# A hybrid block on one core: the order of copies and convolution taps, one buffer moved from the gated outputs to the gates, and a hand-written order for the first and last blocks

## The chip, the cores and the metric

The kernel runs on one NeuronCore of a Trainium2 chip. The metric is the device time in microseconds; a run's time is given as the median of several executions. The engines named below are TensorE (PE, matrix products and transposes), VectorE (DVE), ScalarE (ACT), GpSimd (POOL) and SyncE (SP, which issues most of the DMAs). SBUF is the on-chip memory[...], and PSUM is the memory that matrix products are written to.

## What is computed

Four residual steps on an input x of 4 x 256 rows of 512 columns: attention with an adapter, a feed-forward layer with a selection of rows and columns, a state-space mixer, and the feed-forward layer once more. Nearly all of the time, and all of the change, lies in the mixer and in its seams to the layers before and after it. Of the reference, cut to the mixer:

```python
proj = input_states @ in_proj_w.T                       # gate | x, B, C | dt
gate = proj[..., :INTER]                                # INTER = 128 heads x 64 = 8192
xBC = proj[..., INTER:INTER + CONV]
dt = proj[..., INTER + CONV:]
xBC = silu(depthwise_conv(xBC, conv_w, 4 taps) + conv_b)
hs, Bm, Cm = split(xBC)                                 # 8 groups of B and C, 128 wide
dt = softplus(dt + dt_bias)
cum = cumsum(dt * A)                                    # A = -exp(A_log), one per head
y[i] = sum_{j <= i} (C_i . B_j) * exp(cum_i - cum_j) * dt_j * hs_j  + D * hs_i
g = y * silu(gate)
g = g * rsqrt(mean over the 1024 columns of a group of g*g + eps) * norm_w
out = g @ out_w.T
```

The reference writes the sum over j in chunks with a carried state; the kernel computes it over pieces of 64 rows.

## The kernel before

The 8192 inner columns are cut into 64 blocks of 128 columns, two heads each; eight blocks form a group, which shares one B and one C. All 1024 rows lie along the free axis of a tile, so a block's projection is a 128 x 1024 tile in PSUM. Each float32 product is made from three products of rounded high parts and remainders (`mm3`, lines 115 to 117), so that every weight is split into a high part (a copy on ACT) and a remainder (a subtraction on DVE or POOL).

**One block.** `block(i)` (line 1316) issues, as one step of a software pipeline, work of several blocks. In order of the text:

- the spill of the gated output of block i-2 to DRAM (`spilled`, line 1133), issued from ACT's DMA queue;
- the first half of the projection of x(i) on PE (`projected`, `project`);
- `decays(i-1)`: for two heads, the exponentials of the differences of `cum` on ACT (`exponentials`, line 1070), seven activations each;
- where the projection of B or C for the next group is waiting (blocks 4 and 5 of a group, since `NEXT = {3: "b", 4: "c"}` places these projections at the end of blocks 3 and 4), `conv` of it: a copy with scale and bias on ACT (line 995) and three taps on DVE (line 1002), 1024 columns each, all reading the projection from PSUM;
- `turn(i-1)`: eight transposes of x on PE (line 1096) into two PSUM tiles `trx`, and two copies on DVE into `xd`, multiplied by dt (line 1099); `weigh(i-1)`: the exponentials times the scores, two DVE products `em` (line 1089);
- the second half of x(i), its `conv` on ACT and DVE, the square of block i-2 on ACT and its sum on POOL (`squared`, line 1140);
- `outer`: from group 1 on, a product with the output weights for one tile of 128 rows of the previous group, 24 matmuls into a PSUM tile `pog`;
- silu of x(i) into `x2`, the remainders of the weights fetched, the projection of the gate g(i), the inner products of block i-1 (`product`, 64 small matmuls into `pyy`, and `gated`, lines 1122 to 1131, into a tile `gb`), the differences of block i (`differences`, line 1058, on DVE), and silu of the gate into `gt` (line 1407, ACT).

For ACT, DVE, PE and POOL the loop over the 64 blocks is under `tc.manual_schedule`: each of these engines executes its instructions in exactly the order of the text, one after the other, and an instruction that has to wait holds up all that stands behind it on its engine. SP's DMAs are ordered by the planner. Everything outside that loop is ordered by the planner, which works from its own estimates.

**Buffers.** A tile asked for with a tag takes one of `bufs` buffers, and waits until one is released by all its readers and writers. [...]the projections share two tiles of two banks each (tag `pp`), `pyy` has two banks, and `trx`, `pog` and the scores `pg` share two tiles of one bank each (tag `m` of pool `ps`). In SBUF, B and C after the convolution share the tag `gb` with the gated outputs, four buffers of 128 x 1024; `gt` has one. `em` has three, two being made per block.

**The first blocks.** The projections of dt and of B's first block are made together with the norm before (`first`, line 863). Then lines 911 to 973 compute softplus of dt (exp, a logarithm, and a small series for small values, lines 935 to 938), the running sums `cum` by a scan, store them to DRAM for later loads of single rows (`rows`, line 1045), and transpose `cum`, its suffixes and dt into `col_t`, `end_t` and `dt_t`. Lines 1258 to 1271 follow with the convolutions of B and C of group 0, their scores (`scores`, line 1020: matmuls on PE, masked copies `gm` on DVE) and the first rows. All of this is ordered by the planner together with the first part of block 0.

**The end.** After block 63, lines 1420 to 1441 finish blocks 62 and 63 and the last outer product of group 6, split the output weights of group 7, and begin the output products of the last group for the first four row tiles (`begun`: the half of the sum over blocks 56 to 59). The loop from line 1460 adds the other half, then the feed-forward layer runs. This end is ordered by the planner too.

Of the kernel before, what the change touches and what calls it, by code (L numbers as in the profile page):

```python
# [12 lines left out]
I32 = mybir.dt.int32  # L13
# [66 lines left out]
def hybrid_kernel(  # L80
# [705 lines left out]
    def mixer(feed, later):  # L786
        with ExitStack() as es, ExitStack() as inner:
# [126 lines left out]
            col_t = w1.tile([P, H, TT], F32, name="col_t")  # L914
            end_t = w1.tile([P, H, 4], F32, name="end_t")
            dt_t = w1.tile([P, TT, H], F32, name="dt_t")

            pp = first[0]
            reset = p2.tile([P, NT], F32, name="reset", tag="sq", bufs=1)[:, :512]
            nc.gpsimd.memset(reset, 1.0)  # L920
            nc.gpsimd.memset(reset.rearrange("p (c i) -> p c i", i=P)[:, :, 0:1], 0.0)
            hs = [slice(half * 512, half * 512 + 512) for half in range(2)]
            dtile = lambda n, j: [
                po_.tile([P, 512], F32, name=f"{n}{i}", tag=f"wo{j}", bufs=GB) for i in range(2)
            ]
            vs, es2, lgs, ss = dtile("dv", 0), dtile("de", 0), dtile("dl", 1), dtile("dsr", 1)
            for v, e, h in zip(vs, es2, hs):
                nc.scalar.activation(v, pp[:, h], AF.Identity, bias=dtb_s)
                nc.vector.scalar_tensor_tensor(e, v, -1.0, v, ALU.mult, ALU.min)
            for e in es2:  # L930
                nc.scalar.activation(e, e, AF.Exp)
            for e, lg in zip(es2, lgs):
                nc.scalar.activation(lg, e, AF.Ln, bias=ones[:, 0:1])

            for s, e in zip(ss, es2):
                nc.vector.tensor_scalar(s, e, 1.0 / 3.0, -0.5, ALU.mult, ALU.add)
                nc.vector.tensor_tensor(s, s, e, ALU.mult)
                nc.vector.scalar_tensor_tensor(s, s, 1.0, e, ALU.add, ALU.mult)
            pair = lambda v: v.rearrange("p (k u i) -> p k u i", u=2, i=Q)
            das, natural = dtile("dda", 1), dtile("dc", 0)  # L940
            dts, cums = (p2.tile([P, NT], F32, name=n, tag="x2", bufs=2) for n in ("ddt", "dcum"))
            suf = po_.tile([P, 512], F32, name="dsuf", tag="wo1", bufs=GB)
            for u, (s, e, lg, v, da, nat, h) in enumerate(zip(ss, es2, lgs, vs, das, natural, hs)):
                small = da.bitcast(I32)
                nc.vector.tensor_scalar(small, e, 0.01, None, ALU.is_lt)
                nc.vector.copy_predicated(lg, small, s)
                apart = lambda t: t.rearrange("p (k i) -> p k i", i=Q)
                dt, cum = pair(dts)[:, :, u], pair(cums)[:, :, u]
                nc.vector.scalar_tensor_tensor(dt, apart(v), 0.0, apart(lg), ALU.max, ALU.add)
                nc.vector.tensor_scalar(apart(da), dt, 0.0, a_s, ALU.max, ALU.mult)  # L950
                nc.vector.tensor_tensor_scan(nat, reset, da, 0.0, ALU.mult, ALU.add)
                load(cumd[:, h], nat)
                nc.scalar.copy(cum, apart(nat))

                first_ = apart(nat).rearrange("p (j c) i -> p j c i", j=2)[:, :, :2]
                nc.vector.tensor_tensor(
                    pair(suf).rearrange("p (j c) u i -> p j c u i", j=2)[:, :, :, u],
                    first_[:, :, 1:2, Q - 1 : Q].to_broadcast([P, 2, 2, Q]), first_, ALU.subtract,
                )
            for j in range(2):  # L960
                qs = slice(j * 4, j * 4 + 4)
                tr = ps.tile([P, 4, P], F32, name="trd", tag="m")
                for c in range(4):
# [590 lines left out]
```

## Time and profile before

| | us |
|---|---|
| median of 3 runs | 1909.61 (1905.4 to 1910.39) |
| the profiled execution | 1907.48 |
| its span, first to last instruction | 1905.7 |
| from the first block's gate (block 0) to that of block 8 | 419.2 to 570.7 |
| one group, gate of its first block to that of the next group's (groups 2 to 6) | 181.1 |
| a block with nothing added, gate to gate, in group 3 | 19.79 |
| the blocks behind B and C in group 3, gate to gate | 29.36 and 28.17 |
| last gate (block 63) | 1802.5 |

The profile lists, for every engine, its instructions with start and duration, and for every idle stretch the instruction that ended it. "Gate" is the activation of line 1407, one per block, a handy mark for a block's end. The granted clock is the share of full speed at which TensorE was allowed to run. The lines of the profile that carry the argument are shown in the prediction.

### The profile page before, as it was taken

To read this page: it belongs to the slowest core of one execution; us is meant where nothing else is said; L and a number is where in the kernel's file an instruction comes from. 1 tells how busy PE (TensorE), PEld (TensorE's weight loads), DVE (VectorE), ACT (ScalarE), POOL (GpSimd) and SP (SyncE) were. 2 spreads that over 40 slices of the span, in tenths; PEclk is the share of its full clock that TensorE was granted. 3 is DMA by queue.
4 is the path that set the end of the run, shared out by engine and by line. 5 is a ranking of instruction groups with operands and counts; after the bars stand their busy time and mean duration, and the time that the engine had idled before them with its cause. 6 is when DMAs were issued, how large, how long until landed. Compare 5 with 4: busy or idle time off the path is not lost.

```text
span 1905.7 us, 33071 instructions
## 1 busy us (share of the span) xinstructions
PE 1798.6 (94%) x12882; PEld 1463.3 (77%) x12882; DVE 1449.3 (76%) x2158; ACT 1280.1 (67%) x2520; POOL 246.7 (13%) x251
## 2 busy tenths in 40 slices
PE   7999988889899999999999999999999999999997
PEld 6777767767677778877887888788778877888786
DVE  5566667677787777868886887878778877788776
ACT  6566675467677657766765687578666766776853
POOL 6332230000010111101101110111101011111100
PEclk9999999899999999999999999999999999999999
DMA  4000000112224223432342343234232522343231
GB/s 142 1 1 1 22 15 24 46 56 100 75 93 154 91 82 119 130 100 89 119 135 69 100 154 107 78 96 143 94 94 89 167 88 84 115 135 110 79 113 49
DMA packets 134381, 169.71 MB, mean 89 GB/s; under 512 B 12240, under 2 KB 77392, under 8 KB 134224
## 3 DMA queue, kind: packets, MB, share of 16 engines
q1 hardware_dynamic: 125152, 134.57, 23.2%
q10 hardware_dynamic: 9072, 33.03, 4.5%
q8 instruction: 101, 1.65, 0.4%
q14 instruction: 56, 0.46, 0.1%
HBM read 131.90 MB, written 35.65 MB: 88 GB/s over the span
## 4 chain that ended last, share of the span: by engine, by line
PE 68%; ACT 14%; DVE 13%; issue 3%; POOL 1%; DMA 1%; ACTq 0%; SPq 0%; DVEq 0%; POOLq 0%
PE pp L115 10%; PE pp L116 9%; PE pp L117 9%; PE pyy L1115 7%; PE pog L115 6%; PE pog L116 6%; PE pog L117 6%; DVE bc L1002 3%; ACT em L1076 3%; ACT e L477 2%; PE trx L1096 2%; DVE acc L1002 2%; ACT L1076 1%; DVE em L1089 1%; ACT em L1083 1%
## 5 line engine op out<-in xcount | busy, mean ns | idle before, releaser
L115 PE MATMUL pp<-mx,w 128*128 128x512 f32 (+1 forms) x1160 | 466.5, 402 | 7.7 <-DVE bc L1002 7.2
L117 PE MATMUL pp<-mx,w 128*128 128x512 f32 (+1 forms) x1160 | 454.0, 391 | 5.1 <-DVE w L830 5.1
L116 PE MATMUL pp<-mx,w 128*128 128x512 f32 (+1 forms) x1160 | 453.5, 391 | 0.0
L1148 POOL TENSOR_TENSOR sq<-sq,x 128x1024 f32<-128x1024 f32 x55 | 131.7, 2394 | 1284.1 <-ACT x L1147 1284.1
L1089 DVE TENSOR_TENSOR em<-em,gm 128x1280 f32<-128x1280 f32 x128 | 213.9, 1681 | 87.3 <-ACT em L1084 87.3
L115 PEld LDWEIGHTS pp<-mx,w 128*128 128x128 f32 x1160 | 219.5, 189 | 54.0 <-issue 4.2
L117 PEld LDWEIGHTS pp<-mx,w 128*128 128x128 f32 x1160 | 219.2, 189 | 51.2 <-DVE w L830 5.5
L116 PEld LDWEIGHTS pp<-mx,w 128*128 128x128 f32 x1160 | 219.7, 189 | 40.8 <-issue 0.3
L1002 DVE SCALAR_TENSOR_TENSOR acc<-pp,cw_s,acc 128x1012 f32<-128x1012 f32 (+2 forms) x192 | 244.5, 1273 | 5.1 <-ACT acc L995 0.7
L115 PE MATMUL pog<-wo,gh 128*128 128x512 f32 x512 | 206.4, 403 | 28.8 <-DVE xd L1099 27.4
L116 PE MATMUL pog<-wo,gh 128*128 128x512 f32 x512 | 204.1, 399 | 0.0
L117 PE MATMUL pog<-wo,gh 128*128 128x512 f32 x512 | 203.8, 398 | 0.0
L1014 ACT ACT_TABLE_LOAD x63 | 80.8, 1283 | 164.5 <-DVE acc L1002 164.4
L1407 ACT ACTIVATE gt<-pp 128x1024 f32<-128x1024 f32 x64 | 65.8, 1028 | 175.1 <-PE pp L117 147.3
L1115 PEld LDWEIGHTS pyy<-em,xd 64*64 64x64 f32 x4096 | 136.6, 136 | 54.0 <-DVE em L1089 16.9
L1115 PE MATMUL pyy<-em,xd 64*64 64x256 f32 (+3 forms) x4096 | 166.0, 305 | 11.1 <-DVE em L1089 11.0
L1076 ACT ACTIVATE em<-r,end_t 128x128 f32<-128x128 f32 x512 | 163.3, 389 | 0.8
L1099 DVE TENSOR_TENSOR xd<-trx,dt_t 128x512 f32<-128x512 f32 x128 | 82.3, 685 | 81.8 <-PE trx L1096 81.8
L115 PEld LDWEIGHTS pog<-wo,gh 128*128 128x128 f32 x512 | 98.6, 193 | 54.6 <-DVE xd L1099 32.7
L1002 DVE SCALAR_TENSOR_TENSOR bc<-pp,cw_s,bc 128x1012 f32<-128x1012 f32 (+2 forms) x48 | 61.2, 1275 | 99.6 <-ACT bc L995 98.5
L477 ACT ACTIVATE e<-sc,nmx 128x256 f32<-128x256 f32 (+1 forms) x256 | 104.0, 441 | 21.0 <-DVE nmx L471 20.9
L117 PEld LDWEIGHTS pog<-wo,gh 128*128 128x128 f32 x512 | 98.6, 193 | 21.1
(295 smaller groups left out, 3221.0 us busy)
## 6 DMA issues: line engine op xcount, KB each, us to landing
wr<-in_win_dram SPq DMA_DIRECT2D x145, 256.0 KB, 2.7
r<-cumd SPq DMA_DIRECT2D x256, 128.0 KB, 2.9
spill<-gb ACTq DMA_DIRECT2D x63, 512.0 KB, 2.8
gr<-spill SPq DMA_DIRECT2D x120, 256.0 KB, 3.4
wor<-in_wout_dram SPq DMA_DIRECT2D x64, 256.0 KB, 4.4
out_dram<-x SPq DMA_DIRECT2D x8, 256.0 KB, 2.4
x<-in_x_dram SPq DMA_DIRECT2D x1, 1536.0 KB, 8.7
gr<-spill SPq DMA_DIRECT2D x8, 192.0 KB, 2.6
```

The costliest lines, as they stand in the source:

```text
L115: nc.tensor.matmul(o, lh, rh, start=(first and k == 0), stop=False)
L116: nc.tensor.matmul(o, lh, rl, start=False, stop=False)
L117: nc.tensor.matmul(o, ll, rh, start=False, stop=(last and k == n - 1))
L477: nc.scalar.activation(es_[c][:, 2 * j + pr, :], sc[:, j, :], AF.Exp, bias=nm[:, j : j + 1], accum_out=rs[:, c, h : h + 1],)
L1002: nc.vector.scalar_tensor_tensor(av[:, :, d:], pv[:, :, : L - d], cw_s[:, ch, tap : tap + 1], av[:, :, d:], ALU.mult, ALU.add,)
L1014: nc.scalar.activation(pair(x2).rearrange("p k u i -> p u k i"), acc.rearrange("p (u k i) -> p u k i", u=2, i=Q), AF.Silu,)
L1076: nc.scalar.activation(piece(e, j, c, 2 - c, 2), rv[:, j, 2:, :], AF.Exp, bias=end_t[:, h, 2 * j + c : 2 * j + c + 1],)
L1089: nc.vector.tensor_tensor(e, e, gm, ALU.mult)
L1099: nc.vector.tensor_tensor(xd[:, hs, :].rearrange("p c (h d) -> p c h d", h=2), tr.rearrange("p c (h d) -> p c h d", h=2), dt_t[:, hs, 2 * ...
L1115: nc.tensor.matmul(py[d, u, j * L + c * Q : (j + 1) * L].rearrange("p (k i) -> p k i", i=Q), xd[us, 4 * j + c, d], piece(es2[hh], j, c)[us ...
L1148: (nc.gpsimd if n < NB - 1 else nc.vector).tensor_tensor(sqs[g], sqs[g], x2, ALU.add)
L1407: nc.scalar.activation(gts[i], pp, AF.Silu)
```

## The change

1. **Taps behind the copies.** `conv` is cut into `conv` (the copy on ACT) and `taps` (three operations on DVE). In `block`, the copies of a waiting B or C stay where they were, and their taps come after `turn(i-1)` and `weigh(i-1)`.
2. **Buffers.** Tag `gb` has three buffers, `gt` has two.
3. **The first blocks.** The dt work becomes a generator `steps()` in four parts, which `started()` and block 0 call at fixed places; `started()` and all blocks are under the manual schedule. In block 0 both halves of the gate's projection and the dt transposes come ahead of silu of x; the scores of group 0 move into block 1, and block 1 makes both halves of g(1) before its inner products. Of the small series of dt, one half goes to POOL, and its last operation on two inputs and a constant becomes two operations. `col_t` and `end_t` are laid out with the head as the last axis, so that the copies out of PSUM write in one piece.
4. **The end.** Block 63 makes the last outer product of group 6 after its inner products and ahead of g(63), splits four of the last group's output weights, and loads and splits the first three half tiles of the last group. Then, still under the manual schedule, come the decays, the transposes and the weighing of block 63, the output products `begun` for three row tiles, the other four weights, the inner products of block 63, and the fourth `begun`.

The diff, cut to its core:

```diff
-            col_t = w1.tile([P, H, TT], F32, name="col_t")
-            end_t = w1.tile([P, H, 4], F32, name="end_t")
+            col_t = w1.tile([P, TT, H], F32, name="col_t")
+            end_t = w1.tile([P, 4, H], F32, name="end_t")
...
+            def steps():
...
+                for v, e, h in zip(vs, es2, hs):
+                    nc.scalar.activation(v, first[0][:, h], AF.Identity, bias=dtb_s)
+                    nc.vector.scalar_tensor_tensor(e, v, -1.0, v, ALU.mult, ALU.min)
+                yield
...
+                for s, e, engine in zip(ss, es2, (nc.vector, nc.gpsimd)):
+                    engine.tensor_scalar(s, e, 1.0 / 3.0, -0.5, ALU.mult, ALU.add)
+                    engine.tensor_tensor(s, s, e, ALU.mult)
+                    engine.tensor_scalar(s, s, 1.0, None, ALU.add)
+                    engine.tensor_tensor(s, s, e, ALU.mult)
+                yield
...
+                yield
+                for v, n, end, func in ((cums, 4, col_t, AF.Copy), (suf, 2, end_t, AF.Copy), (dts, 4, dt_t, AF.Relu)):
+                    for j in range(2):
+                        tr = ps.tile([P, n, P], F32, name="trd", tag="m")
...
+                        nc.scalar.activation(end[:, n * j : n * j + n, :], tr, func)
+                yield
...
-                    else po_.tile([P, NT], F32, name="bc", tag="gb", bufs=4)
+                    else po_.tile([P, NT], F32, name="bc", tag="gb", bufs=3)
                 )
                 nc.scalar.activation(
                     acc, pp, AF.Identity, bias=cb_s[:, ch : ch + 1], scale=cw_s[:, ch, 3:4]
                 )
+                return acc
+
+            def taps(acc, pp, ch):
+
                 av = acc.rearrange("p (b t) -> p b t", b=B)
...
+            def started():
+
+                prepare(2)
+                next(dt_steps)
+                pieces.pop(0)
+                group["b"] = conv(first[1], NB, False)
+                taps(group["b"], first[1], NB)
+                next(dt_steps)
+                prepare(3)
+                fetch(6)
+                pp = whole(projected("c", 0))
+                group["c"] = conv(pp, NB + G, False)
+                silu(group["b"])
+                next(dt_steps)
+                taps(group["c"], pp, NB + G)
+                rr.update((h, rows(h)) for h in range(2))
...
                 for k in waiting:
-                    group[k] = conv(group.pop(k + "pp"), (NB if k == "b" else NB + G) + g + 1, False)
+                    group[k] = conv(group[k + "pp"], (NB if k == "b" else NB + G) + g + 1, False)
+                if i == 1:
+                    next(x_steps)
+                    scoring = scores(group.pop("b"), group.pop("c"))
+                    gms[0] = next(scoring)
+                    for _ in scoring:
+                        pass
                 if i:
                     turn(i - 1)
                     weigh(i - 1)
-                acc = conv(next(x_steps), i, True)
+                for k in waiting:
+                    taps(group[k], group.pop(k + "pp"), (NB if k == "b" else NB + G) + g + 1)
+                if i != 1:
+                    next(x_steps)
+                acc = conv(pp, i, True)
+                taps(acc, pp, i)
...
+                g_steps = projected("g", i)
+                if i == 0:
+                    pp = whole(g_steps)
+                    next(dt_steps)
+                    silu(group["c"])
                 xs2[i] = side_by_side(acc)
...
+                both = i == NB - 1
+                if i:
                     next(g_steps)
-                if i:
+                    if not done:
+                        pp = next(g_steps)
+                    if i == 1:
+                        next(g_steps)
                     inner_products(i - 1)
-                if done:
-                    next(g_steps)
+                    if both:
+                        done = outer(G - 2, TT - 1)
+                    if done:
+                        pp = next(g_steps)
...
+                if both:
+                    scaled(*done)
+                    for k in range(4):
+                        upper_out(g * GB + k)()
+                    begin(0)
+                    begin(1)
+                    begin(2)
...
-                gts[i] = p2.tile([P, NT], F32, name="gt", tag="gt", bufs=1)
+                gts[i] = p2.tile([P, NT], F32, name="gt", tag="gt", bufs=2)
...
+            def begin(t):
+                begins[t] = parts(G - 1, t, 0)
...
+                started()
                 for i in range(NB):
                     block(i)
...
+                es_p.close()
+                ps_o = pool("m_o", 4, space=PSUM, **freed)
+                i = NB - 1
+                spilled(i - 1, gbs[i - 1])
+                decays(i)
+                turn(i)
+                weigh(i)
+                for t in range(3):
+                    begun(t)
+                begin(3)
+                lower = [upper_out(i - 3 + k) for k in range(4)]
+                squared(i - 1, xs2.pop(i - 1), gbs.pop(i - 1))
+                inner_products(i)
+                for f in lower:
+                    f()
+                spilled(i, gbs[i])
+                squared(i, xs2.pop(i), gbs.pop(i))
+                begun(3)
```

## The prediction, made before the changed kernel was run

> **What bounds the kernel now.** I read first the page's busy line and its chain, then the list of what TensorE (PE) waited for in each stage of the mixer, then one block in order of time on PE, VectorE (DVE) and ScalarE (ACT), and last the granted clock in the stretches after those waits.
>
> ```profile
> PE 1798.6 (94%) x12882; PEld 1463.3 (77%) x12882; DVE 1449.3 (76%) x2158; ACT 1280.1 (67%) x2520; POOL 246.7 (13%) x251
> ...
> PE 68%; ACT 14%; DVE 13%; issue 3%; POOL 1%; DMA 1%; ACTq 0%; SPq 0%; DVEq 0%; POOLq 0%
> ```
>
> PE holds the chain over most of the span. In the mixer (436 to 1790 us) its waits are few and of one kind:
>
> ```profile
> PE pog L115 <- DVE xd L1099: 27.1, 12, 2.6
> PE pyy L1115 <- DVE em L1089: 8.7, 7, 2.0
> PE pp L115 <- DVE bc L1002: 7.2, 2, 3.8
> ```
>
> Columns: total us, times, longest. The twelve are two per group in groups 1 to 6: the block behind the projection of B and the block behind that of C. Here is one (group 3, behind C): DVE first, then PE.
>
> ```profile
> 1036.36 3.90 DVE L1002 SCALAR_TENSOR_TENSOR bc<-pp,cw_s,bc 128x1012 f32<-128x1012 f32 x3 [7.16 <-ACT bc L995]
> 1040.17 1.28 DVE L1099 TENSOR_TENSOR xd<-trx,dt_t 128x512 f32<-128x512 f32 x2
> 1041.37 4.80 DVE L1089 TENSOR_TENSOR em<-em,gm 128x1280 f32<-128x1280 f32 x2
> 1046.09 3.89 DVE L1002 SCALAR_TENSOR_TENSOR acc<-pp,cw_s,acc 128x1012 f32<-128x1012 f32 x3
> ...
> 1038.30 0.39 PE L117 MATMUL pp<-mx,w 128*128 128x512 f32 x1
> 1040.91 0.50 PE L115 MATMUL pog<-wo,gh 128*128 128x512 f32 x1 [2.22 <-DVE xd L1099]
> ```
>
> DVE stands idle for 7.16 us at the head of the taps of C, because ACT comes to C's copy (L995) only after the fourteen activations of two heads' decays. The copies of x (xd) are queued behind those taps although their transposes ended at 1035.9. The output product needs a PSUM buffer that only xd frees, so PE stops.
>
> The stop costs more than itself:
>
> ```profile
> 985.00:1000.00 15.00, 15.00 (x120) 12.21 (x120) 13.41 (x17) 9.42 (x12) 2.41 (x1) 1.00 0.35 110
> 1011.00:1019.00 8.00, 7.46 (x28) 5.75 (x32) 7.96 (x6) 2.15 (x4) 2.38 (x1) 0.79 0.00 0
> 404.00:409.00 5.00, 0.55 (x3) 0.13 (x1) 5.00 (x8) 0.25 (x1) 0.00 (x0) 0.94 0.29 105
> 409.00:416.00 7.00, 6.10 (x21) 4.29 (x21) 2.66 (x5) 2.77 (x5) 0.00 (x0) 0.56 0.31 112
> ```
>
> The third number from the right is the granted PE clock: 1.00 in a dense stretch, 0.79 behind the wait at 1009 us, 0.56 behind an idle of 5.1 us at the start. After the wait the 24 output matmuls took 7.3 us in six of the twelve blocks and 5.67 us in the other six.
>
> **What the Trainium skill says.** "TensorE: Matmul & The Clock Gate", What's actually happening: the clock goes to half after an idle window, read in free-running windows of about 3.4 us, so it depends on where the wait falls. The trace agrees: 7.3 against 5.67 us behind the same 2.2 us wait. "SBUF — State Buffer", SBUF: two separate sides: a DVE operation with two SBUF inputs and a GpSimd (POOL) operation exclude each other for a whole instruction. The trace agrees: two em products take 2.9 us alone and 4.80 above, where POOL's square sum of 2.4 us runs; the taps, with one PSUM input, stay at 1.28. "ScalarE: Activation LUTs", What ACT_TABLE_LOAD costs: 1283 ns for the load and about as much for a drain. The trace has the 1283 and no drain beside it (load 420.25 to 421.53, next activation at 421.54), so 1.28 is used.
>
> **The change part by part.** The sum is made against the profiled run: 1907.5 us, its span 1905.7; the median of the three is 1909.6, 2.1 above, within their spread of 5.
>
> *Middle: taps behind the copies, groups 1 to 6.* DVE now does xd (1.28), em, em (1.49 each), then the three taps of C (3.85), then those of x. With the times above: xd 1035.6 to 1036.9, the first em to 1038.4, the second (its exponential ended at 1035.2) to 1039.9, C's taps to 1043.8, x's taps to 1047.7 (was 1050.0). The em products now end before POOL's sum starts (1041). PE runs on: output product 1038.7 to 1044.2, pyy to 1046.6, then the gate projection, which needs the PSUM buffer that C's taps give back at 1043.8: 2.8 us to spare. In place of the projection waiting 2.2 us nothing is late; at B's block the same sum gives the buffer at 1014.2 against a need at 1017.1. PE alone needs 25.24 us from gate to gate here (a plain block of 19.79 plus 24 matmuls at 0.2275). It took 29.3 and 27.75. So 4.1 + 2.5 = 6.6 us per group, of which 4.5 is waiting and 1.6 the half clock; six groups 39.6. I take 38, because a restart of 0.1 to 0.2 us may remain. Below: 27, the waits alone; 15 if another wait takes half their place.
>
> *Group 0.* It has no output product to fill PE; one block takes 16.38 us and runs in a ring: exponentials 5.34, em 1.58, taps 3.85, table and silu 2.3, w 0.5, wait 0.33 for gb, gate silu 1.03, table 1.28, and 0.17 of gaps. Two gate buffers remove the 0.33 in about five blocks: 1.7. In blocks 4 and 5 (behind B, C) the taps of x end 2.5 to 3.9 us earlier, but B's and C's taps end 1.6 later (483.3 against 481.7), and PE's gate projection waits for them: 3.3 and 3.85 us now, 4.8 and 4.9 then. PE sets the gate there: without a clock loss the two blocks gain 2 together, with half clock behind both (the skill's window is shorter than such a wait; the second has 0.76 already) they lose 2 to 3. I take -0.7, sum +1; bounds -4 and +4. The gate's other waits for gb (27.8 us of ACT in all) are hidden by PE and cost nothing.
>
> *Start.* The dt work is cut into four steps in the order of the text, and the blocks follow it. Walking DVE from its start at 386.9 with the rows' durations: de to 388.7, B's taps 392.6, one half of the small series 394.6 (its twin of four operations goes to POOL: two of 1.29 and two bounded by 0.5 (a memset) and 1.3, done by 396.2 at the latest, needed at 398), the two halves of step 3 to 401.4, C's taps 405.2, x's 409.0, w 409.6, differences 411.6. PE: c, x(0), g(0) back to back to 404.2, then twenty transposes in six groups; ACT evacuates them by 408.0 (col_t and end_t are now written in one piece: 0.6 as dt_t, not 1.0), then silu of C and x, w, gate at 411.6 (was 420.2), exponentials to 418.2 (was 426.9). Of the 8.7 some goes back, since the score products move into block 1 between x's projection and the transposes: PE x(1) 409.7 to 415.2, scores to 418.4, xd 420.6, em 423.5, taps of x(1) 427.3 against 432.2. Gain 4.9. POOL's prepare(3) stands behind its four operations and ends at 397.5; g(0) needs it at 398.7. SP must store the scan and load two rows between 401 and 409.6: 2.0 + 2.9 us. If PE's sparse transposes bring the half clock, x(1) costs 2.5 more. I take 4.5; bounds 0 and 8.
>
> *End.* The last outer product moves ahead of g(63), and 36 output matmuls stand before pyy(63). Before: PE waited 0.35, 1.32 and 2.22, and pyy ran at a clock of 0.50, 4.54 us instead of 2.4; the group's square sums began at 1828.4. New, from pyy(62) at 1795.25: outer to 1800.8, g to 1806.3, transposes 1807.2, three half products 1815.4. ACT's gate is queued behind the third load of spilled rows (its buffer comes back at 1805, 3.4 us to land): 1808.8, exponentials to 1816.4, em 1818.0, so pyy ends at 1820.4. The fourth half product ends at 1823.1; gb and four weight remainders end at 1825.6, the square sum at 1826.8. 1.6 earlier; I take 1.5; bounds -6 (two waits at half clock) and +5.
>
> *The rest.* gb with three buffers: while B and C hold two, gb(4) takes the third, from gb(3), whose square ends at 1040.9 and whose spill lands 2.8 us after 1027; it is written after 1050. Nothing. The new layout of col_t and end_t is read through the same counts of elements: nothing.
>
> Sum: 38 + 1 + 4.5 + 1.5 = 45. **1907.5 - 45 = 1862.5; I forecast 1862.**
>
> **Rivals.** *A, half the wait comes back under another name* (em, or the PSUM buffer of B and C, with 2.8 us to spare): the middle gives 15, so 1907.5 - 22 = 1885.5. For it: two em products against POOL's sum could cost 1.8 each. Against: in the walk they end 1.1 us before POOL starts. *B, start and end in fixed order lose what the middle gives:* start -3, group 0 -4, end -3, middle 38: 1879.5. For it: waits of 4.8 us on PE in blocks 4 and 5, and ACT's gate behind a load at the end. Against: the walks above. *C, slower:* B's and C's projections hold their PSUM buffer so long that the gate projection waits in all fourteen blocks. It starts to cost at 2.8 us over my walk and eats everything at about 6.6 over; at 9 us over, 12 x 2.9 = 35 us, less 7 for the rest, 1935. For it: group 0 shows that very wait (7.2 us). Against: there PE had no output product in between. *D, the buffers were no real limit and PE still waits:* about 1905; against it, the transposes end 4 us before xd.
>
> **Numbers.** Forecast 0.63, A 0.14, B 0.12, C 0.08, D 0.03. The range 1848 to 1883 holds the forecast's bounds (middle 27 to 40, start 0 to 8, end -6 to 5, not all at their worst) and B, and about half of A. About 0.3% (6 us) can be told from no change: faster 0.88, same 0.03, slower 0.09.
>
> **What would show it.** The row pog <- xd should vanish from PE's waits, the blocks behind B and C take 25.3 us from gate to gate, the group 174.5 instead of 181.1, with a clock of 1.00. The first gate silu should fall at 411 to 414. A wait of pp <- bc in groups 1 to 6 would make A or C right; the gate of block 5 later than its distance to block 3 before (50.1 us) would make B right.

## The result: 1875.25 us, and where the 33 us come from

The changed kernel takes 1875.25 us (median of four runs, 1874.66 to 1875.91); the kernel before took 1908.63 beside it (1905.40 to 1910.39). The ratio is 0.9827, with a 95% interval from 0.9810 to 0.9844: 33 us faster. The forecast was 1862, with a range from 1848 to 1883. The profiled execution has a span of 1874.1 us against 1905.7 before, 31.6 less, and the table below accounts for these 31.6.

From the page after, the busy line and the shares of the chain:

```profile
PE 1792.8 (96%) x12882; PEld 1463.0 (78%) x12882; DVE 1428.6 (76%) x2156; ACT 1275.4 (68%) x2518; POOL 252.1 (13%) x255
...
PE 80%; DVE 8%; ACT 7%; issue 2%; POOL 1%; DMA 1%; SPq 0%; DVEq 0%; ACTq 0%; POOLq 0%
```

PE has 12 points more of the chain, DVE and ACT have 5 and 7 fewer. The two longest rows of PE's waits in the mixer say why (total us, times, longest):

```profile
PE pp L115 <- DVE bc L1006: 9.8, 2, 4.9
PE pyy L1118 <- DVE em L1092: 7.8, 4, 2.0
```

The first row of before, twelve waits of the output product for `xd` with 27.1 us in all, is gone. In groups 1 to 6 nothing new stands in its place, and from gate 8 to gate 56 the granted clock is 1.00. The row that was third, the gate projection waiting for the taps of B and C, has grown from 7.2 to 9.8 us; both its waits are in group 0.

Here is the place that the prediction walked, group 3 behind C, first on DVE, then on PE (the first matmul of each run of equal ones):

```profile
1024.02 1.29 DVE L1102 TENSOR_TENSOR xd<-trx,dt_t 128x512 f32<-128x512 f32 x2 [5.40 <-PE trx L1099]
1025.23 2.88 DVE L1092 TENSOR_TENSOR em<-em,gm 128x1280 f32<-128x1280 f32 x2
1028.03 3.90 DVE L1006 SCALAR_TENSOR_TENSOR bc<-pp,cw_s,bc 128x1012 f32<-128x1012 f32 x3
1031.84 3.89 DVE L1006 SCALAR_TENSOR_TENSOR acc<-pp,cw_s,acc 128x1012 f32<-128x1012 f32 x3
```

```profile
1027.00 0.39 PE L115 MATMUL pog<-wo,gh 128*128 128x512 f32 x1
1032.53 2.41 PE L1118 MATMUL pyy<-em,xd 64*64 64x256 f32 x64
1034.87 0.50 PE L115 MATMUL pp<-mx,w 128*128 128x512 f32 x1
```

`xd` now comes first, and its idle time is a wait for the transposes, which is work that PE does then. The output product starts without a bracket, so it waited for nothing. The taps of C end at 1031.93 (1028.03 and 3.90), and the gate projection needs their buffer at 1034.87: 2.9 us to spare, where the walk had 2.8. The two `em` products take 2.88 together in place of 4.80, since POOL's square sum (1029.49 to 1031.9) now lies beside the taps. That saving on DVE is not what ends PE's stop: before, PE had no wait for `em` behind B or C (between gate 8 and gate 56 it had two, at 577 and 580 us). The gate's activation shows the pace; the three rows are blocks 3, 4 and 5 of group 3:

```profile
990.19 1.03 ACT L1442 ACTIVATE gt<-pp 128x1024 f32<-128x1024 f32 x1 [3.74 <-PE pp L117]
1015.42 1.03 ACT L1442 ACTIVATE gt<-pp 128x1024 f32<-128x1024 f32 x1 [0.74 <-PE pp L117]
1040.65 1.03 ACT L1442 ACTIVATE gt<-pp 128x1024 f32<-128x1024 f32 x1 [1.02 <-PE pp L117]
```

From gate to gate 25.23 and 25.23 us, against 29.36 and 28.17 before; the prediction had 25.24 as the time that PE alone needs.

The gates cut the whole mixer into stages. The marks are the start of dt's first activation (`dv`), of the gate of block 1, of block 8 (the first of group 1), of block 56 (the first of the last group), and the end. All in us, from the profiled executions:

| Stage | before | after | gain | the prediction's term |
|---|---|---|---|---|
| start of the span to `dv` | 386.2 | 388.9 | -2.7 | none |
| `dv` to gate 1 (start) | 49.4 | 50.5 | -1.1 | +4.5 |
| gate 1 to gate 8 (group 0) | 135.1 | 138.0 | -2.9 | +1 |
| gate 8 to gate 56 (middle) | 1089.6 | 1048.8 | +40.8 | +38 |
| gate 56 to the end (end) | 245.4 | 247.9 | -2.5 | +1.5 |
| sum | 1905.7 | 1874.1 | +31.6 | +45 |

Up to `dv` the two programs do the same work. Over the fourteen profiled executions of this study `dv` starts anywhere between 386.0 and 389.8; the two ends of this range are two programs below that differ only from block 4 on. So the first row is taken as chance, and the times below are read from `dv` on. Three of the four parts that the change touches come out lower than forecast, and the one that carries the gain comes out higher.

### The profile page after: what moved, and what is told of

It reads as the page before. It is cut to its first block, busy times and chain, and to the rows that moved or that the text cites. A ratio compares the mean times of both kernels' runs of the same rounds, so it can differ in the third digit from the quotient of the medians.

```text
span 1874.1 us, 33084 instructions
## 1 busy us (share of the span) xinstructions
PE 1792.8 (96%) x12882; PEld 1463.0 (78%) x12882; DVE 1428.6 (76%) x2156; ACT 1275.4 (68%) x2518; POOL 252.1 (13%) x255
## 4 chain that ended last, share of the span: by engine, by line
PE 80%; DVE 8%; ACT 7%; issue 2%; POOL 1%; DMA 1%; SPq 0%; DVEq 0%; ACTq 0%; POOLq 0%
PE pp L115 14%; PE pp L117 13%; PE pp L116 13%; PE pyy L1118 8%; PE pog L115 6%; PE pog L117 6%; PE pog L116 6%; PE trx L1099 3%; ACT e L477 2%; PE ptr L493 1%; PE pq L115 1%; PE pg L1036 1%; DVE acc L1006 1%; PE pq L116 1%; PE pq L117 1%
## 5 line engine op out<-in xcount | busy, mean ns | idle before, releaser
L1006 DVE SCALAR_TENSOR_TENSOR acc<-pp,cw_s,acc 128x1012 f32<-128x1012 f32 (+2 forms) x192 | 244.6, 1274 | 7.2 <-ACT acc L995 2.6
L1092 DVE TENSOR_TENSOR em<-em,gm 128x1280 f32<-128x1280 f32 x128 | 188.7, 1489 | 70.8 <-ACT em L1087 70.8
L115 PE MATMUL pog<-wo,gh 128*128 128x512 f32 x512 | 202.3, 395 | 2.3 <-ACT gh L1209 1.3
L117 PE MATMUL pog<-wo,gh 128*128 128x512 f32 x512 | 200.8, 392 | 0.8 <-DVE gh L1214 0.8
L116 PE MATMUL pog<-wo,gh 128*128 128x512 f32 x512 | 200.3, 392 | 0.0
L115 PEld LDWEIGHTS pog<-wo,gh 128*128 128x128 f32 x512 | 96.8, 189 | 22.8 <-ACT gh L1209 1.8
L117 PEld LDWEIGHTS pog<-wo,gh 128*128 128x128 f32 x512 | 96.7, 189 | 21.4 <-DVE gh L1214 1.1
L116 PEld LDWEIGHTS pog<-wo,gh 128*128 128x128 f32 x512 | 96.8, 189 | 19.5
```

The source lines that it names most:

```text
L115: nc.tensor.matmul(o, lh, rh, start=(first and k == 0), stop=False)
L116: nc.tensor.matmul(o, lh, rl, start=False, stop=False)
L117: nc.tensor.matmul(o, ll, rh, start=False, stop=(last and k == n - 1))
L1006: nc.vector.scalar_tensor_tensor(av[:, :, d:], pv[:, :, : L - d], cw_s[:, ch, tap : tap + 1], av[:, :, d:], ALU.mult, ALU.add,)
L1092: nc.vector.tensor_tensor(e, e, gm, ALU.mult)
```

## The experiments

The theory after the result: the order of the taps alone makes the gain. Start, group 0 and end each give something back: the start to a small series split over DVE and POOL and to PE at half clock, group 0 to the half clock behind its two waits, the end to a load that is queued ahead of the last gate. The rival: the parts need one another (without the second gate buffer or the fixed order the middle would gain less), and the missing 13 us are chance or lie elsewhere.

### The taps alone

```diff
                 for k in waiting:
-                    group[k] = conv(group.pop(k + "pp"), (NB if k == "b" else NB + G) + g + 1, False)
+                    group[k] = conv(group[k + "pp"], (NB if k == "b" else NB + G) + g + 1, False)
                 if i:
                     turn(i - 1)
                     weigh(i - 1)
-                acc = conv(next(x_steps), i, True)
+                for k in waiting:
+                    taps(group[k], group.pop(k + "pp"), (NB if k == "b" else NB + G) + g + 1)
+                pp = next(x_steps)
+                acc = conv(pp, i, True)
+                taps(acc, pp, i)
```

The rest is as in the kernel before (with `conv` cut in two): start, end, four buffers `gb`, one `gt`.

> The kernel before, with nothing changed but the place of the taps of B and C behind the copies of x. Theory (the order alone gives the middle, 40 us; group 0 pays back 3 to 4): 1871 to 1873, and the row pog <- xd gone from the waits of TensorE. Rival (the two gate buffers are needed for it, since the gate would still wait for gb): 1882 or more, with a new wait in groups 1 to 6.

Measured: 1867.27 us, ratio 0.9793 (0.9779 to 0.9808). That is about 4 us below the expected range. Gate 8 to gate 56 takes 1048.1 us, the gain of the full change and 0.7 more. The two longest rows of PE's waits in the mixer:

```profile
PE pp L115 <- DVE bc L1006: 9.8, 2, 4.9
PE pyy L1119 <- DVE em L1093: 9.0, 6, 2.2
```

The twelve waits for `xd` are gone here too; one of 0.3 us is left, at the end. The move of the taps is the whole gain, and all the rest of the change together costs 6.5 us by the two ratios, 8 by the medians. From `dv` on: start 49.2 (after 50.5), group 0 136.8 (138.0), end 244.6 (247.9). Not all of this is the order: block 3's gate to block 5's took 51.8 us here and 53.9 in the full change, with the same two waits of 4.9 us in both. Behind them the granted clock was 0.79 and 0.75 here (8.0 and 8.5 us), 0.63 and 0.67 there.

### The buffers alone

```diff
-                    else po_.tile([P, NT], F32, name="bc", tag="gb", bufs=4)
+                    else po_.tile([P, NT], F32, name="bc", tag="gb", bufs=3)
...
-                gb = po_.tile([P, NT], F32, name="gb", tag="gb", bufs=4)
+                gb = po_.tile([P, NT], F32, name="gb", tag="gb", bufs=3)
...
-                gts[i] = p2.tile([P, NT], F32, name="gt", tag="gt", bufs=1)
+                gts[i] = p2.tile([P, NT], F32, name="gt", tag="gt", bufs=2)
```

> The kernel before with three buffers for gb and two for gt. Theory (the gate's waits for gb are hidden but for 0.33 us in some blocks of group 0): 1906 to 1908, the twelve waits pog <- xd unchanged at 2.2. Rival (they carry a part of the middle): 1900 or less. Slower by over 2 us would mean that the third gb buffer is missed.

Measured: 1907.3 us, ratio 0.9996 (0.9988 to 1.0005), no change that can be measured. In the profile the plain blocks of group 0 come 15.95 apart in place of 16.38, the 0.43 of which the prediction counted 0.33. That is 1.3 us from gate 0 to gate 8, less than the interval can tell. The middle stays at 1089.7.

### How much of the wait was clock

The kernel before, with nine extra matmuls ahead of the output product in the blocks behind B and C. They run in PE's wait, nobody reads them, and they are work added.

```diff
+                if waiting and g:
+                    warmed(ps_y.tile([P, NT], F32, name="warm", tag="pyy")[:, :512], [xs[0][:, 0, :P].bitcast(F32)] * 9)
                 done = outer(*out) if out and not first_out else None
```

> The kernel before with nine small matmuls, whose results nobody reads, put on TensorE into each of the twelve waits of 2.2 us. Theory (six of the twelve waits trip the clock to half, 1.6 us each): 1898 to 1900, and all twelve output products at 5.6 to 5.7 us. Rival (the 7.3 us of six of them are not from the clock): 1908 to 1910, six at 7.3 still.

Measured: 1902.6 us, ratio 0.9965 (0.9952 to 0.9978), a gain, but less than the expected 1898 to 1900. The waits shrink, since PE works through most of their time:

```profile
PE pog L115 <- DVE xd L1099: 5.0, 12, 0.6
```

All twelve output products now take 5.66 to 5.70 us, where six had taken 7.3, so those were slow by the clock. The blocks still end when `xd` lets them: about 28.16 and 27.75 from gate to gate in every group. The middle takes 1081.9 in place of 1089.6. So the half clock behind the waits was 7.7 us of the stage, where 10 had been worked out: the six products give 9.7 back, but the block after the one behind C, which had made up 0.4 a group, no longer does. The other 33 of the 40.8 go with the wait itself: these blocks are still 2.7 us on average over the 25.23 of the full change, of which nine matmuls of 0.23 and the 0.4 of wait that is left make 2.5.

### Group 0: the order, or the clock

First the order. The full change, with the taps of B and C ahead of the copies in group 0 alone, as before:

```diff
                     group[k] = conv(group[k + "pp"], (NB if k == "b" else NB + G) + g + 1, False)
+                    if not g:
+                        taps(group[k], group.pop(k + "pp"), (NB if k == "b" else NB + G) + g + 1)
...
                 for k in waiting:
-                    taps(group[k], group.pop(k + "pp"), (NB if k == "b" else NB + G) + g + 1)
+                    if g:
+                        taps(group[k], group.pop(k + "pp"), (NB if k == "b" else NB + G) + g + 1)
```

> The changed kernel, but in group 0 the taps of B and C ahead of the copies again. Theory (in group 0 the later taps hold the PSUM buffer, TensorE waits 4.9 us and falls to half clock): block 3's gate to block 5's 50 us instead of 53.9, time 1871 to 1872. Rival (the new order helps the other engines there as well, so giving it up costs as much): 1875 or more.

Measured: 1870.67 us, ratio 0.9812 (0.9792 to 0.9832); the interval overlaps that of the full change, and the stage tells more. Gate 1 to gate 8 takes 134.6 in place of 138.0. PE's waits there are 2.90 and 3.87 long, where the full change has 4.91 twice.

Then the clock. The full change with twenty extra matmuls, which nobody reads, in each of those two waits:

```diff
+                if waiting and not g:
+                    warmed(ps.tile([P, C], F32, name="warm", tag="m"), [xs[0][:, 0, :P].bitcast(F32)] * 20)
                 g_steps = projected("g", i)
```

> The changed kernel with twenty small matmuls, whose results nobody reads, in TensorE's waits of 4.9 us in blocks 4 and 5 of group 0. Theory (half of what group 0 lost is the half clock behind these waits): clock 1.00 behind them, block 3's gate to block 5's at 50 to 51 us instead of 53.9, time 1871.5 to 1873. Rival (the wait itself is the loss): 1875.

Measured: 1866.97 us, ratio 0.9778 (0.9762 to 0.9794), with gate 1 to gate 8 in 132.5 us. This is 2.1 less than with the old order, although the taps come as late as in the full change. Full change first, PE's wait and then the stretches of 8.0 and 8.5 us behind the two waits (sums of PE, PEld, DVE, ACT, POOL; the third number from the right is the granted clock):

```profile
487.08 0.77 PE L115 MATMUL pp<-mx,w 128*128 128x512 f32 x1 [4.91 <-DVE bc L1006]
```

```profile
487.00:495.00 8.00, 7.92 (x77) 5.84 (x77) 4.26 (x4) 3.79 (x4) 0.00 (x0) 0.63 0.13 35
514.50:523.00 8.50, 8.32 (x78) 6.25 (x79) 4.78 (x6) 3.79 (x4) 0.00 (x0) 0.67 0.11 34
```

The same with the extra matmuls, each of which is two records in the trace:

```profile
479.98 4.63 PE L122 MATMUL warm<-mx,ones 128*128 128x128 f32 x40
485.05 0.47 PE L115 MATMUL pp<-mx,w 128*128 128x512 f32 x1 [0.45 <-DVE bc L1006]
```

```profile
485.00:493.00 8.00, 7.95 (x88) 6.41 (x89) 6.77 (x7) 3.80 (x4) 0.00 (x0) 1.00 0.11 33
510.00:518.00 8.00, 8.00 (x88) 6.40 (x89) 6.74 (x8) 3.80 (x4) 0.00 (x0) 1.00 0.11 36
```

The gate projection begins when the taps allow it in both; what differs is the pace behind it. Block 3's gate to block 5's takes 48.7 us in place of 53.9. So 5.2 us of group 0 were half clock in the full change's profile. What the old order would take there at full clock wasn't tried, so how much the later taps cost by themselves stays open.

### The start

Three runs. First the small series on DVE alone, three operations a half, as before (the rest as in the full change):

```diff
-                for s, e, engine in zip(ss, es2, (nc.vector, nc.gpsimd)):
-                    engine.tensor_scalar(s, e, 1.0 / 3.0, -0.5, ALU.mult, ALU.add)
-                    engine.tensor_tensor(s, s, e, ALU.mult)
-                    engine.tensor_scalar(s, s, 1.0, None, ALU.add)
-                    engine.tensor_tensor(s, s, e, ALU.mult)
+                for s, e in zip(ss, es2):
+                    nc.vector.tensor_scalar(s, e, 1.0 / 3.0, -0.5, ALU.mult, ALU.add)
+                    nc.vector.tensor_tensor(s, s, e, ALU.mult)
+                    nc.vector.scalar_tensor_tensor(s, s, 1.0, e, ALU.add, ALU.mult)
```

> The changed kernel with the whole small series of dt on VectorE, in three operations a half as before, none on GpSimd. Theory (GpSimd's four operations and the weight split behind them hold VectorE up by about as much as they relieve it): within 1 us of the changed kernel, 1874 to 1875.5, the running sums of the second half no later than 22 us after the first dt activation. Rival (moving half of the series away is a gain): 1877.

Measured: 1873.14 us, ratio 0.9804 (0.9787 to 0.9821); the interval overlaps that of the full change. The trace tells more than the time. In the full change the two engines stand in one another's way, DVE first, then POOL:

```profile
397.83 1.66 DVE L944 TENSOR_TENSOR dsr<-dsr,de 128x512 f32<-128x512 f32 x1
399.41 1.51 DVE L951 TENSOR_SCALAR dda<-de 128x512 int32<-128x512 f32 x1
...
404.74 0.42 DVE L951 TENSOR_SCALAR dda<-de 128x512 int32<-128x512 f32 x1
```

```profile
395.94 1.58 POOL L943 TENSOR_SCALAR dsr<-dsr 128x512 f32<-128x512 f32 x1
397.60 1.34 POOL L944 TENSOR_TENSOR dsr<-dsr,de 128x512 f32<-128x512 f32 x1
398.90 1.74 POOL L108 TENSOR_TENSOR w<-wr,w 128x512 fp32r<-128x512 f32 x1
```

The comparison at L951 takes 0.42 us alone and 1.51 beside POOL's split of weights. From the start of `de` to the start of C's taps DVE needs 19.3 us in the full change and 18.7 with both halves on DVE. Giving one half to POOL saved DVE nothing: the four operations of the other half took 4.15 us on DVE (395.26 to 399.41), six operations for both halves 4.7, and the slow comparison cost 1.1 more. With both halves on DVE, `dv` to gate 1 takes 49.7 us in place of 50.5.

Second, the clock. Eleven extra matmuls ahead of dt's transposes and eight ahead of the projection of x(1), read by nobody:

```diff
+                warmed(ps.tile([P, C], F32, name="warm", tag="m"), [xs[0][:, 0, :P].bitcast(F32)] * 11)
                 for v, n, end, func in ((cums, 4, col_t, AF.Copy), (suf, 2, end_t, AF.Copy), (dts, 4, dt_t, AF.Relu)):
...
-                next(x_steps)
+                pp = next(x_steps)
+                if i == 1:
+                    warmed(pp, [xs[0][:, 0, :P].bitcast(F32)] * 8)
```

> The full change with extra matmuls whose result nobody reads in two waits of TensorE at the start: eleven (2.5 us) ahead of dt's transposes, eight (1.9 us) ahead of x(1)'s projection. Theory (the start missed its forecast partly because dt's transposes and x(1) ran at half clock): x(1)'s matmuls behind the wait for w take 5.0 us in place of 6.9, dt's first activation to gate 1 falls from 50.5 to about 48.5 us, the run by 2 us. Rival (the chain over VectorE and ScalarE sets gate 1 and TensorE's clock there costs nothing): 50.5 us stays, no gain.

Measured: 1872.61 us, ratio 0.9806 (0.9784 to 0.9828). The stretch between dt's transposes and x(1), full change and then this run:

```profile
409.00:417.00 8.00, 5.08 (x22) 3.54 (x22) 7.86 (x8) 5.98 (x11) 0.00 (x0) 0.62 0.18 68
```

```profile
409.00:417.00 8.00, 6.44 (x49) 5.10 (x47) 7.83 (x8) 6.02 (x10) 0.00 (x0) 1.00 0.27 90
```

x(1)'s matmuls behind the wait for `w` take 5.3 us in place of 7.1, and `dv` to gate 1 falls from 50.5 to 48.7, as the theory had it. (The two places were filled in one run, so how the 1.8 us divide between the transposes and x(1) isn't shown apart.) Against the full change the median is 2.6 lower, but the intervals overlap; the stage mark carries the reading.

Third, the start of the kernel before in the full change, with everything else kept:

```diff
-                started()
                 for i in range(NB):
                     block(i)
```

(with the lines that `started` and the two first blocks replaced put back, and the taps behind the copies as in the first run).

> The full change with the start of the kernel before: dt's steps, the scores and the first two blocks placed by the planner as before, the small series on VectorE. Theory (the hand-written start costs, not gains): dt's first activation to gate 1 takes 49.2 us in place of 50.5, and group 0's gates come 16.38 apart; about 1872 us, 1 to 3 faster than the full change. Rival (the start written by hand gains the 4.5 us that the forecast gave it, and the loss lies elsewhere): 1878 us or more.

Measured: 1871.78 us, ratio 0.9807 (0.9791 to 0.9823), overlapping the full change again. `dv` to gate 1 takes 48.8, gate 1 to gate 8 takes 136.6. The new start reaches gate 0 earlier (29.3 us behind `dv` in place of 32.8), and has lost all of it and 1.7 more by gate 1.

### The end

First the load. The full change with the begin of the third half product behind the gate and the decays of the last block:

```diff
                     begin(0)
                     begin(1)
-                    begin(2)
...
-                for t in range(3):
+                for t in range(2):
                     begun(t)
+                begin(2)
+                begun(2)
                 begin(3)
```

> The changed kernel with the third load of spilled rows (and its split) behind the decays of block 63 instead of ahead of its gate. Theory (the gate of block 63 waits 9.15 us on ScalarE behind that load, and the whole end after it): gate 63 at 1767, the square sums of the last group 2 to 4 us earlier, 1871.5 to 1873.5. Rival (TensorE has its half products to fill the time, so the wait costs nothing): 1875.

Measured: 1873.25 us, ratio 0.9808 (0.9792 to 0.9823). The gate of block 63, full change first, then this run:

```profile
1775.34 0.62 ACT L1209 CAST gh<-gr 128x512 fp32r<-128x512 f32 x1 [9.15 <-DMA gr<-spill]
...
1775.87 1.02 ACT L1442 ACTIVATE gt<-pp 128x1024 f32<-128x1024 f32 x1
```

```profile
1770.69 1.03 ACT L1441 ACTIVATE gt<-pp 128x1024 f32<-128x1024 f32 x1 [6.21 <-PE pp L117]
```

The gate comes 25.2 us behind that of block 62 in place of 28.7, and the stage takes 246.3 in place of 247.9. Of 3.5 us at the gate 1.6 are left at the end.

Second, the end as the planner lays it out, in the full change:

```diff
-                es_p.close()
-                ps_o = pool("m_o", 4, space=PSUM, **freed)
-                i = NB - 1
...
+            i = NB - 1
+            spilled(i - 1, gbs[i - 1])
+            decays(i)
...
+            es_p.close()
+            ps_o = pool("m_o", 4, space=PSUM, **freed)
```

> The changed kernel with the end of the kernel before, in the planner's order. Theory (the order of the text at the end lost 2.5 us against the planner's): 1872 to 1873.5. Rival (the end is no worse than before, and the 2.5 us come from the clock's windows by chance): 1875 or more.

Measured: 1873.6 us, ratio 0.9811 (0.9795 to 0.9827). Gate 56 to the end takes 245.1 us, 2.8 less than in the full change, which undoes the 2.5 of the table. The intervals of both runs overlap that of the full change; here too it is the stages that tell them apart.

### The parts that are worth something, together

The taps alone and the extra matmuls of group 0, on the start, buffers and end of before:

```diff
+                if waiting and not g:
+                    warmed(ps.tile([P, C], F32, name="warm", tag="m"), [xs[0][:, 0, :P].bitcast(F32)] * 20)
                 g_steps = projected("g", i)
```

> The kernel before with two changes only: the taps of B and C behind the copies of x (start, buffers and end as before), and twenty extra matmuls whose result nobody reads in each of the two 4.9 us waits of group 0 (extra work, 4.6 us of TensorE in each). Theory (the order gives the middle, the half clock behind the two waits gives group 0, and planner's start and end are no worse than those written by hand): from the taps-only run's marks, block 3's gate to block 5's falls from 51.8 to 48.7 us, the rest stays: about 1864 us median. Rival (the 5.5 us that the same extra matmuls gave in the full change came from somewhere else, or the taps-only run had its clock by chance): 1867 or more.

Measured: 1865.22 us, ratio 0.9772 (0.9756 to 0.9788). Block 3's gate to block 5's takes 48.3 us; from `dv` to the end 1475.0, against 1478.7 with the taps alone and 1485.2 in the full change. The last run adds the change's buffers to this:

```diff
-                    else po_.tile([P, NT], F32, name="bc", tag="gb", bufs=4)
+                    else po_.tile([P, NT], F32, name="bc", tag="gb", bufs=3)
...
-                gts[i] = p2.tile([P, NT], F32, name="gt", tag="gt", bufs=1)
+                gts[i] = p2.tile([P, NT], F32, name="gt", tag="gt", bufs=2)
```

> The parts that the runs found worth something, together: the kernel before with the taps of B and C behind the copies of x, the change's buffers (gb three, gt two), and the twenty extra matmuls, whose result nobody reads, in each of the two waits of group 0; start and end as before. Theory (parts add up): group 0's blocks come 15.96 apart in place of 16.38, so gate 1 comes 0.4 earlier after dt's first activation and gate 8 about 1 earlier after gate 1 than in the run without the change's buffers: dt's first activation to the end 1473.5 us in place of 1475.0, about 1863.5 us median, ratio 0.9765. Rival (the buffers are worth nothing in group 0 either, as in the kernel before): 1865, ratio 0.9772.

Measured: 1864.7 us over five runs, ratio 0.9762 (0.9747 to 0.9776). Group 0 gains as expected: `dv` to gate 1 in 48.8 in place of 49.2, gate 1 to gate 8 in 132.5 in place of 133.4. The middle gives 0.9 of it back (1048.9 against 1048.0) and the end 0.6, so the time from `dv` to the end is 1475.2: the parts don't add up to more, and the buffers stay worth nothing that can be measured. By the ratios both versions beat the full change by 10 to 12 us. Their extra matmuls are work that the computation doesn't need; of the versions without them, the taps alone are the fastest that was run.

## Why the prediction was right, and where its sum failed

**The middle: mechanism and size right.** Taps behind the copies free `xd`, `xd` frees the output product, PE runs through. The term was 38 of a worked-out 39.6; 40.8 were measured in the full change, 41.5 with the taps alone. The prediction read the block behind C as 27.75 us; the gates give 28.17, and the next block makes 0.42 of it up, so its 6.6 a group stands (181.1 to 174.4 measured). The split into 4.5 us of waiting and 1.6 of half clock a group was right in kind: the extra matmuls took back 7.7 us of the clock's 10. One agreement was claimed too easily: it sets a window of about 3.4 us beside these waits, and waits of 2.2 us are shorter than that. The runs show that half clock came behind some of them and that filling them ended it; the length of a window they don't show. Of the two causes that rivals A and C named, neither came: `em` no longer meets POOL, and the buffer of B and C had 2.9 us to spare, where rival C needed less than none.

**The start: the step that failed most, 5.6 us.** The prediction walked DVE from `de` to C's taps in 14.5 us; it took 19.3. Three terms were too small. "One half of the small series" was set at 2.0 and took 4.15: four operations come to 2.2 at the durations that they have with POOL at rest (0.42 and 0.69 each, in the run with the series on DVE), and the rest is POOL's operations, counted only as POOL's own time, which held up DVE. The comparison behind it took 1.51 for 0.4. And "the two halves of step 3 to 401.4" was summed too low: the rows of before give 3.9 a half, 7.9 in all with no gap between them, and the prediction had 6.8; the run shows 8.4 without the slow comparison. Together they make up the 4.8 that was missing there. The half clock at x(1), which the prediction named and put into its bounds at 2.5, came too and cost 1.8 by the run with extra matmuls. The bound of 0 below was not low enough: -1.1.

The Trainium skill had the collision. "SBUF — State Buffer", Who interferes with whom, says that VectorE shares a port pair with GpSimd, that VectorE instructions with two SBUF inputs contend with GpSimd's reads, and that `tensor_scalar` can as well, in a mode that uses both ports. The prediction applied it to the `em` products, where it helped, and not to the series, where the change put both engines on SBUF at once. The trace agrees in the times: 0.42 us alone, 1.51 beside POOL.

**Group 0: the bound came instead of the value.** The waits were forecast at 4.8 and 4.9 us and are 4.91 and 4.91. The prediction said that with half clock behind both the two blocks lose 2 to 3, and took -0.7. They lost 3.8 (50.1 to 53.9), more than that. The term that was mis-sized is the chance of the clock: a wait of 4.9 us was put between a loss and none. In the seven programs without extra matmuls that have these two waits, the loss is 1.7 to 3.9, and never none. With the wait filled, these two blocks gain 1.4 on the kernel before (48.7 against 50.1), close to the 2 that it gave "without a clock loss".

**The end: +1.5 forecast, -2.5 measured.** The walk was nearly good as far as the gate. It had gate 63 at 1808.8 in the times of before, which is 1774.7 here when set at gate 62 of both (1781.2 and 1747.2); it came at 1775.87, 1.1 late. Most of what it missed stands behind the gate, on PE and then on DVE and POOL:

```profile
1776.94 0.50 PE L115 MATMUL pog<-wo,gh 128*128 128x512 f32 x1 [0.96 <-ACT gt L1442]
1785.21 3.33 PE L1118 MATMUL pyy<-em,xd 64*64 64x256 f32 x62 [1.94 <-DVE em L1092]
```

```profile
1787.98 2.49 DVE L1214 TENSOR_TENSOR gh<-gr,gh 128x384 fp32r<-128x384 f32 x1 [2.23 <-ACT gh L1209]
1790.39 1.39 DVE L1130 SCALAR_TENSOR_TENSOR gb<-x,dh,pyy 128x512 f32<-128x512 f32 x2
```

```profile
1787.69 2.37 POOL L1151 TENSOR_TENSOR sq<-sq,x 128x1024 f32<-128x1024 f32 x1 [28.16 <-ACT x L1150]
```

The half products wait 0.96 us for the gate, which the prediction didn't have, but that delays nothing by itself, since `pyy` behind them waits 1.94 for `em` all the same. `em` comes 1.2 late, about as the gate did, and `pyy` then runs 3.33 us for a usual 2.4. It ends at 1788.5, where the walk, set to these times, had 1786.3. Then DVE, in the order of the text, waits for a load's copy ahead of `gb` and is slowed by POOL's square sum, so that `gb` begins at 1790.39, 1.9 us after `pyy` could be read. The sums begin at 1797.0; the walk had the square sum end at 1792.7. So the steps that failed are `pyy` at its usual pace and DVE free for `gb`, with 1.0 and 1.9 us, and the gate with 1.2.

**The rest.** 2.7 us lie ahead of all that was changed, and are taken as chance. With the 5.6 of the start, 3.9 of group 0 and 4.0 of the end, less the 2.8 by which the middle was better, they are the 13.4 between the forecast gain and the measured one. The range held because the middle carries nearly all of the gain; each of the other three terms had the wrong sign. Rival B, start, group 0 and end losing what the middle gives, is what came: it had -3, -4 and -3, measured -1.1, -2.9 and -2.5, and its time of 1879.5 is nearer to 1875.25 than the forecast's 1862. Its price for the waits in blocks 4 and 5 and for a gate behind a load was written down beside it; it got 0.12, because the walks of the likeliest case were trusted more than the waits they passed. Against the profiled 1905.7, the three parts gave back 6.5 us where 7 of gain had been counted.

## What to carry to other kernels

Move the consumer that frees a buffer ahead of the work that can wait, and try that move alone first: here the move of the taps gave 41 us, and all the rest of the change around it cost 6.5 to 8. When a fixed order is planned, price the clock behind every wait that PE keeps, and count each operation given to POOL on DVE's time too, where both read SBUF. A stage mark inside the trace (here the gates) resolves 1 to 3 us that medians with a spread of 4 us leave open.

## What the runs showed of the hardware that was not expected

- A wait of PE also costs behind it. In group 0, two waits of 4.9 us brought granted clocks of 0.63 and 0.67 over the following 8.0 and 8.5 us, and the two blocks took 5.2 us longer than with twenty matmuls inside each wait, where the clock was 1.00 over 8 us and the waiting itself was no shorter.
- The same order met the clock differently from program to program (one profiled execution of each): with the same two waits of 4.9 us, block 3's gate to block 5's took 53.9, 54.0, 53.8, 52.8, 52.4, 51.9 and 51.8 us in seven programs without the extra matmuls, and 48.7, 48.3 and 48.7 in the three with them.
- A program's start is not a fixed mark. With the same work ahead of it, `dv` began between 386.0 and 389.8 us in fourteen executions, a spread larger than most of the effects looked for here.
